# Four layers over 32 sequences: how the output of the state-space scan is multiplied by C and summed

## The chip, the cores and the metric

The kernel runs on one core of a Trainium2 chip. Its time is the device time of one execution in microseconds (us). A core has five engines that run side by side, each with its own queue that it works off in order: TensorE (PE; its weight loads are listed as PEld), VectorE (DVE), ScalarE (ACT), GpSimd (POOL) and SyncE (SP, which here only issues transfers). They wait for each other through semaphores. TensorE writes its products to PSUM, which this kernel deals out in eight banks of 512 float32 on each of 128 partitions; the other working memory is SBUF. The profile lists the clock that TensorE was granted as a share of full speed.

## The reference, cut to what matters

32 sequences (B) of 256 tokens (S) with 256 channels (D) go through four layers: a linear attention, an ordinary attention with 16 heads, a state-space layer run over time in both directions, and another linear attention. All is float32. The change is in the third layer, whose core is this:

```python
def _ssm(u, Wdbc, Wdt, bdt, Alog, Dp):           # u: 256 steps, E = 512 channels
    dlt, Bm, Cm = jnp.split(einsum(u, Wdbc), [R, R + N], axis=-1)   # R = 64, N = 16
    delta = softplus(einsum(dlt, Wdt) + bdt)
    dA  = exp(delta[..., None] * -exp(Alog))                        # N states a channel
    dBu = delta[..., None] * Bm[:, :, None, :] * u[..., None]
    h_t = dA_t * h_{t-1} + dBu_t                                    # scan over the 256 steps
    y_t = sum over n of h_t[:, n] * C_t[n]
    return y + u * Dp
...
out = (silu(mx) * (z1 + z2)) @ Wf.T + bf + skip      # z1 forward, z2 backward in time
return x + gate[:, None, :] * out
```

## The kernel before, in words

**Tiling.** Channels lie on partitions in the scans: 512 channels are 4 chunks of 128, and a tile [128, 4, 256] holds (channel, chunk, time), 1024 elements a partition. For each sequence b and direction d, `project(b, d)` makes `u`, `dbc` (64 rows for delta, then 16 rows of B and 16 of C), `dl` (delta) and `du` (delta times u). Then `scan(b, d)` takes N = 16 steps, one for each state n. So there are 32 x 2 x 16 = 1024 steps.

**One step.** TensorE copies row n of B and row n of C to all partitions (L574: two float32 matmuls with a selecting 32-row matrix, into one PSUM bank `bc`; there are two such banks). ScalarE computes `dA` with four exponentials (L580). VectorE then does three operations on 1024 elements: `du` times B (L585), the scan, a recurrence along the free dimension (L586), and the product with C in place (L587). In every odd step VectorE also adds the even step's `h` (L592), and TensorE adds the pair's sum into PSUM with an identity matrix (L594, two float32 matmuls of 512 columns, tile `ys`). After 16 steps VectorE reads the sum (L601). Each of the two `h` tiles has one buffer, so the next `h` of the same parity waits for the add and the matmul.

**What runs beside.** Two chains of other work are interleaved with the steps, by Python generators: one unit of `back(b - 1)` (the end of the state-space layer and the last layer, for the sequence before) and two of `ahead(b)` (`project(b, 1)` and then `front(b + 1)`, the first two layers and the start of the third for the next sequence). A scheduler of the framework then places the instructions in each engine's queue by its own estimate of times, so the order in a queue is not exactly that of the source. The scan of a sequence's first direction can't begin before `front` of that sequence has ended. The chains share three PSUM banks, `psG` (`bank()`); the sums of the second layer's heads, `yv` (L454), have a bank of their own, `psV`. Both chains use GpSimd for the reciprocal root in each layer norm (`stats`, L220 and L221), and for little else.

**Names that the text uses.** `ys` L594: identity matmuls that sum h; `bc` L574: broadcast of B and C; `yv` L454 and the logits L415 and L445: the second layer's heads, with 17 columns or 18 rows a matmul; `rs` L220: the norms' roots on GpSimd; L638 to L640: in `back`, the skip `xs` is added, the gate multiplied, `x` added.

Of the kernel before, what the change touches and what calls it, by code (L numbers as in the profile page):

```python
# [30 lines left out]
# Vectors that lie along the free dimension, three on each of four partitions.  # L31
# [4 lines left out]
def cond_seq_kernel(ctx: ExitStack, tc: tile.TileContext, a: dict, out: bass.AP):  # L36
    nc = tc.nc
    PSUM = bass.MemoryType.PSUM

    const = ctx.enter_context(tc.tile_pool(name="const", bufs=1))  # L40
    xin = ctx.enter_context(tc.tile_pool(name="xin", bufs=2))
    small = ctx.enter_context(tc.tile_pool(name="small", bufs=4))
# [46 lines left out]
    with tc.tile_pool(name="pre", bufs=1) as pre:  # L89
# [34 lines left out]
        # silu(cond), and its transpose  # L124
# [5 lines left out]
        ps = bank()  # L130
# [5 lines left out]
        # Half of each FiLM's scale and shift, with its norm's own folded in.  # L136
# [21 lines left out]
        # shift, scale and gate of the state space layer, a batch element a partition  # L158
# [7 lines left out]
        mod = const.tile([B, 3, D], F32, name="mod")  # L166
# [6 lines left out]
        # What the masks add to keys, and what they multiply values by.  # L173
        mb = const.tile([B, 3, S], F32, name="mb")
# [10 lines left out]
        ps = bank()  # L185
# [9 lines left out]
    # Tiles of which a part is set once and for all.  # L195
# [110 lines left out]
        # Where every key is masked, exp gives zeros and their sum's inverse no number.  # L306
# [17 lines left out]
        # queries: softmax over a head's channels, its division left to the end  # L324
# [50 lines left out]
    def attention(ch, x, b, dst):  # L375
        xT = yield from norm_T(ch, x, "ng1", "nb1")
        # A head's 16 channels of 32 partitions; row 16 pairs 1 (q) with the mask's term (k),
        # row 17 the negated maximum (q, later) with 1 (k).
        kpat = small.tile([B, P], F32, tag="kpat", name="kpat", bufs=2)
# [59 lines left out]
        for h in range(16):  # L439
            g, j = divmod(h, 4)  # L440
            hh, h8 = divmod(h, 8)
            r = slice(32 * j, 32 * j + 18)
            ps = bank()
            for m in range(2):
                nc.tensor.matmul(  # L445
                    ps[:, m * 256 : (m + 1) * 256], ka[r, g, m * P : (m + 1) * P], qa[r, g, :], start=True, stop=True
                )
            ex = wk.tile([P, 2, S], F32, tag="ex", name="ex", bufs=3)
            nc.scalar.activation(ex.rearrange("p m s -> p (m s)"), ps, AF.Exp)  # L449
            if h8 == 0:  # L450
# [13 lines left out]
            yield  # L464
# [4 lines left out]
    def front(b):  # L469
        """Layers 0 and 1, and layer 2 up to the first direction's scan."""  # L470
# [7 lines left out]
        # layer 2: norm, scale and shift, norm  # L478
        sel = ident[0:B, b : b + 1].to_broadcast([B, P])
# [3 lines left out]
        xs = wk.tile([P, 2, D], F32, tag="xs", name="xs")  # L483
# [7 lines left out]
        xn = stats("f", xs)  # L491
        yield
# [21 lines left out]
        state[b] = {"x": x2, "xs": xs, "gate": gate, "xT": xT, "mz": mz}  # L514
        yield from project(b, 0)

    def project(b, d):
        """What the scan of a direction reads; the second direction's time runs backwards."""
# [22 lines left out]
        nc.scalar.copy(dbc, ps[:96, :256])  # L541
        yield
        # softplus(z) = max(z, 0) + ln(1 + exp(-|z|))
# [20 lines left out]
        state[b][d] = (u, dbc, dl, du)  # L564
        yield

    def scan(b, d):
        u, dbc, dl, du = state[b].pop(d)
        yp = psY.tile([P, 2, 512], F32, tag="y", name="ys")
        for n in range(N):  # L570
            bc = psB.tile([P, 2, S], F32, tag="bc", name="bc")
            for i in range(2):
                o = R + i * N + n
                nc.tensor.matmul(  # L574
                    bc[:, i, :], ident[R:96, o : o + 1].to_broadcast([32, P]), dbc[R:96, :], start=True, stop=True
                )
# [8 lines left out]
            nc.vector.tensor_tensor(h, du, bc[:, 0:1, :].to_broadcast([P, 4, S]), ALU.mult)  # L585
            nc.vector.tensor_tensor_scan(hf, dA.rearrange("p c s -> p (c s)"), hf, 0.0, ALU.mult, ALU.add)  # L586
            nc.vector.tensor_tensor(h, h, bc[:, 1:2, :].to_broadcast([P, 4, S]), ALU.mult)  # L587
            # y sums over n: pairs here, the pairs in PSUM.
            if n % 2 == 0:
                even = h  # L590
            else:
                nc.vector.tensor_tensor(h, h, even, ALU.add)  # L592
                for i in range(2):
                    nc.tensor.matmul(  # L594
                        yp[:, i, :], ident, hf[:, i * 512 : (i + 1) * 512], start=n == 1, stop=n == N - 1
                    )
            yield
# [12 lines left out]
    def back(b):  # L610
        """Layer 2 from the scans on, and layer 3."""
# [30 lines left out]
        xo = wk.tile([P, 2, D], F32, tag="xo", name="xo")  # L642
# [12 lines left out]
    for b in range(B):  # L655
        # Two chains beside the scans: what remains of the last element, and the next one's start.
# [18 lines left out]
def _arrays(i):  # L675
    """The inputs as the program reads them: the same values, laid out anew."""
# [74 lines left out]
```

## Time and profile before

| | |
|---|---|
| time before, median of 3 runs | 9736.15 us (9734.44 to 9742.32) |
| the profiled execution, first to last instruction | 9737.5 us |
| PE matmul busy | 8259.0 us (85%), 27390 instructions |
| VectorE busy | 6998.2 us (72%) |
| ScalarE busy | 3321.2 us (34%) |
| GpSimd busy | 407.5 us (4%) |
| granted TensorE clock, mean | 0.693 |

One sequence takes 300 us, and the work repeats: the stretch from 4000 to 4100 us and that from 4300 to 4400 us have nearly the same busy times. In the lists of groups each row gives the line, the engine, the operation, what it writes and reads, how often, then the busy time in us, the mean of one in ns, and the idle time of the engine just before, with what ended most of it. PE busy is a modelled figure: matmuls overlap, so the spacing of their starts is the better measure of what one costs.

### The profile page before, as it was taken

The numbers are of one execution on the slowest core, as the hardware profiler recorded it, in microseconds if no ns is written. First come the engines' busy times: TensorE is split into PE (matmuls) and PEld (weight loads), VectorE is DVE, ScalarE is ACT, GpSimd is POOL, SyncE is SP. The second block draws the span as 40 slices with busy tenths as digits, with TensorE's granted clock in tenths as the row PEclk, the third lists the DMA queues.
The fourth block names the chain that finished last, engine by engine and source line by source line (L and its number), as shares of the span: only waits on it lengthen the run. The fifth ranks groups of instructions, "written<-read, shape, count | busy, mean of one in ns | idle before, by whom it ended". The sixth has DMA issues, their size and how long they took to land.

```text
span 9737.5 us, 73176 instructions
## 1 busy us (share of the span) xinstructions
PE 8259.0 (85%) x27390; PEld 5211.9 (54%) x27390; DVE 6998.2 (72%) x7756; ACT 3321.2 (34%) x7236; POOL 407.5 (4%) x557
## 2 busy tenths in 40 slices
PE   6888888888888888888888888888888888888886
PEld 4555555555555555555555555555555555555553
DVE  1777777777777777777777777777777777777776
ACT  1333332333333333323333333333233333333332
POOL 0000000000000000000000000000000000000000
PEclk6677676776666776767766667767677766677675
DMA  1000000000000000000000000000000000000000
GB/s 58 2 3 2 2 3 3 3 2 3 2 3 3 3 2 2 3 3 3 2 3 2 3 3 3 2 2 3 3 3 3 2 2 3 3 3 0 2 2 2
DMA packets 28172, 34.67 MB, mean 4 GB/s; under 512 B 3781, under 2 KB 23557, under 8 KB 27818
## 3 DMA queue, kind: packets, MB, share of 16 engines
q1 hardware_dynamic: 23024, 24.51, 0.8%
q10 hardware_dynamic: 4794, 5.49, 0.2%
q8 instruction: 217, 3.56, 0.2%
q14 instruction: 137, 1.12, 0.0%
HBM read 21.60 MB, written 8.39 MB: 3 GB/s over the span
## 4 chain that ended last, share of the span: by engine, by line
PE 66%; DVE 26%; ACT 3%; issue 2%; POOL 2%; DMA 0%; DVEq 0%; ACTq 0%; SPq 0%; POOLq 0%
PE ys L594 14%; DVE h L586 9%; PE yv L454 8%; PE g L256 7%; PE bc L574 7%; PE g L445 6%; DVE h L585 5%; PE g L257 4%; DVE h L587 4%; PE g L415 3%; PE g L390 3%; PE g L526 2%; PE g L235 2%; PE g L299 1%; PE g L550 1%
## 5 line engine op out<-in xcount | busy, mean ns | idle before, releaser
L580 ACT ACTIVATE dA<-dl,alog 128x255 f32<-128x255 f32 x4096 | 1768.0, 497 | 2320.3 <-DVE h L586 2319.8
L586 DVE TENSOR_TENSOR_SCAN h<-dA,h 128x1024 f32<-128x1024 f32 x1024 | 2337.9, 2283 | 25.4 <-ACT dA L580 1.4
L574 PE MATMUL bc<-dbc,ident 32*128 32x256 f32 x4096 | 1715.9, 553 | 682.4 <-DVE h L587 625.5
L585 DVE TENSOR_TENSOR h<-du,bc 128x1024 f32<-128x1024 f32 x1024 | 1241.6, 1212 | 1071.8 <-PE ys L594 595.5
L594 PE MATMUL ys<-h,ident 128*128 128x512 f32 x2048 | 1665.1, 957 | 301.8 <-DVE h L592 301.8
L574 PEld LDWEIGHTS bc<-dbc,ident 32*128 32x128 f32 x4096 | 967.5, 260 | 1101.1 <-issue 592.2
L587 DVE TENSOR_TENSOR h<-h,bc 128x1024 f32<-128x1024 f32 x1024 | 1240.4, 1211 | 5.8
L594 PEld LDWEIGHTS ys<-h,ident 128*128 128x128 f32 x2048 | 545.1, 296 | 1017.7 <-issue 534.6
L454 PEld LDWEIGHTS yv<-va,ex 128*128 128x128 f32 x4096 | 777.1, 283 | 348.2 <-ACT ex L449 173.3
L454 PE MATMUL yv<-va,ex 128*128 128x17 f32 x4096 | 791.7, 335 | 82.9 <-ACT ex L449 82.8
L449 ACT ACTIVATE ex<-g 128x512 f32<-128x512 f32 x512 | 294.6, 595 | 1188.0 <-PE g L445 1119.8
L415 PE MATMUL g<-ka,qa 18*128 18x256 f32 x2048 | 592.4, 569 | 78.3 <-DVE b L350 55.4
L592 DVE TENSOR_TENSOR h<-h 128x1024 f32<-128x1024 f32 x512 | 619.3, 1210 | 5.7
L445 PE MATMUL g<-qa,ka 18*128 18x256 f32 x2048 | 620.7, 557 | 0.0
L220 POOL TENSOR_SCALAR rs<-mv 128x2 f32<-128x2 f32 x256 | 204.2, 798 | 8791.9 <-DVE mv L219 8791.9
L257 PE MATMUL g<-rows,ones 1*128 1x256 f32 x1152 | 538.2, 556 | 0.0
L415 PEld LDWEIGHTS g<-ka,qa 18*128 18x128 f32 x2048 | 369.5, 269 | 235.3 <-DVE b L350 67.4
L526 PE MATMUL g<-mz,w_wc 128*128 128x256 f32 x2048 | 454.0, 380 | 0.0
L557 DVE TENSOR_SCALAR dl<-g,cols 128x256 f32<-128x256 f32 x256 | 119.9, 479 | 424.6 <-ACT ab L556 420.2
L526 PEld LDWEIGHTS g<-mz,w_wc 128*128 128x128 f32 x2048 | 390.1, 191 | 53.8 <-issue 0.6
L235 PE MATMUL g<-ident,f 128*128 128x128 f32 x896 | 216.3, 369 | 214.9 <-DVE f L224 116.3
L257 PEld LDWEIGHTS g<-rows,ones 1*128 1x128 f32 x1152 | 223.0, 240 | 266.1 <-issue 265.9
(180 smaller groups left out, 8501.5 us busy)
## 6 DMA issues: line engine op xcount, KB each, us to landing
x<-in_x_dram SPq DMA_DIRECT2D x32, 256.0 KB, 2.7
out_dram<-xo SPq DMA_DIRECT2D x32, 256.0 KB, 2.1
fw<-in_film_dram SPq DMA_DIRECT2D x3, 1024.0 KB, 10.0
wada<-in_wada_dram ACTq DMA_DIRECT2D x1, 1536.0 KB
w_wc<-in_wc_dram ACTq DMA_DIRECT2D x1, 1024.0 KB, 11.9
w_wc<-in_wc_dram SPq DMA_DIRECT2D x1, 1024.0 KB, 14.3
w_wv<-in_wv_dram ACTq DMA_DIRECT2D x2, 256.0 KB, 7.5
w_wo<-in_wo_dram ACTq DMA_DIRECT2D x2, 256.0 KB, 10.1
```

The costliest lines, as they stand in the source:

```text
L256: nc.tensor.matmul(o, xT[:, k, t * P : (t + 1) * P], w[:, k, :], start=k == 0, stop=False)
L257: nc.tensor.matmul(o, brow[1][:, :P], brow[0], start=False, stop=True)
L415: nc.tensor.matmul(ps[:, t * 256 : (t + 1) * 256], qa[r, g, t * P : (t + 1) * P], ka[r, g, :], start=True, stop=True)
L445: nc.tensor.matmul(ps[:, m * 256 : (m + 1) * 256], ka[r, g, m * P : (m + 1) * P], qa[r, g, :], start=True, stop=True)
L454: nc.tensor.matmul(yp[:, t, h8, :], ex[:, m, t * P : (t + 1) * P], va[:, m, h, :], start=m == 0, stop=m == 1)
L526: nc.tensor.matmul(ps[:, j * 256 : (j + 1) * 256], wc[d][:, k, e * P : (e + 1) * P], mz[:, k, :], start=k == 0, stop=k == 3,)
L574: nc.tensor.matmul(bc[:, i, :], ident[R:96, o : o + 1].to_broadcast([32, P]), dbc[R:96, :], start=True, stop=True)
L580: nc.scalar.activation(dA[:, c, 1:S], dl[:, c, 1:S], AF.Exp, bias=0.0, scale=aneg[d][:, c, n : n + 1])
L585: nc.vector.tensor_tensor(h, du, bc[:, 0:1, :].to_broadcast([P, 4, S]), ALU.mult)
L586: nc.vector.tensor_tensor_scan(hf, dA.rearrange("p c s -> p (c s)"), hf, 0.0, ALU.mult, ALU.add)
L587: nc.vector.tensor_tensor(h, h, bc[:, 1:2, :].to_broadcast([P, 4, S]), ALU.mult)
L594: nc.tensor.matmul(yp[:, i, :], ident, hf[:, i * 512 : (i + 1) * 512], start=n == 1, stop=n == N - 1)
```

## The change

C no longer goes through TensorE. `project` writes the 16 rows of C to a scratch in DRAM (`cd`), and `scan` reads two rows at a time back, repeated on all partitions, into an SBUF tile `cc` with three buffers. The product with C moves to GpSimd. `bc` now holds the two B rows of two steps, so there is one pair of broadcast matmuls for two steps, in a single bank. VectorE's product of `du` and B goes to a PSUM tile of two banks (`dbu`), and the scan reads it there. VectorE's add of pairs is gone: TensorE sums all 16 steps. `h` has three buffers in rotation. PSUM is dealt anew: `psB` has one bank instead of two, `psV` is gone and `yv` takes one of the three shared banks.

Smaller edits: `mod` and `mb` share one tile, on partitions 32 to 63 and 0 to 31; the buffers of `xs`, `xo`, `kpat` and of the small statistics are cut by one; and `front` now adds gate times `xs` to `x2` on GpSimd, so that `back` has two VectorE operations where it had three.

```diff
-    psB = ctx.enter_context(tc.tile_pool(name="psB", bufs=2, space=PSUM))
-    psV = ctx.enter_context(tc.tile_pool(name="psV", bufs=1, space=PSUM))
+    psB = ctx.enter_context(tc.tile_pool(name="psB", bufs=1, space=PSUM))
+    psU = ctx.enter_context(tc.tile_pool(name="psU", bufs=1, space=PSUM))
+    dram = ctx.enter_context(tc.tile_pool(name="dram", bufs=2, space=bass.MemoryType.DRAM))
...
-                yp = psV.tile([P, 2, 8, 17], F32, tag="v", name="yv")
+                yp = bank()[:, : 2 * 8 * 17].rearrange("p (t h d) -> p t h d", t=2, h=8)
...
         xn = stats("f", xs)
+        nc.gpsimd.tensor_tensor(xs, xs, gate.unsqueeze(1).to_broadcast([P, 2, D]), ALU.mult)
+        nc.gpsimd.tensor_tensor(x2, x2, xs, ALU.add)
...
+        cd = dram.tile([N, S], F32, tag="cd", name="cd")
+        nc.sync.dma_start(out=cd, in_=dbc[R + N : R + 2 * N, :])
...
         for n in range(N):
-            bc = psB.tile([P, 2, S], F32, tag="bc", name="bc")
-            for i in range(2):
-                o = R + i * N + n
-                nc.tensor.matmul(
-                    bc[:, i, :], ident[R:96, o : o + 1].to_broadcast([32, P]), dbc[R:96, :], start=True, stop=True
-                )
+            if n % 2 == 0:
+                cc = big.tile([P, 2, S], F32, tag="cc", name="cc", bufs=3)
+                nc.sync.dma_start(out=cc, in_=cd[n : n + 2, :].partition_broadcast(P))
+                bc = psB.tile([P, 2, S], F32, tag="bc", name="bc")
+                for i in range(2):
+                    o = R + n + i
+                    nc.tensor.matmul(
+                        bc[:, i, :], ident[R:96, o : o + 1].to_broadcast([32, P]), dbc[R:96, :], start=True, stop=True
+                    )
...
-            h = big.tile([P, 4, S], F32, tag=f"h{n % 2}", name="h", bufs=1)
+            h = big.tile([P, 4, S], F32, tag="h", name="h", bufs=3)
             hf = h.rearrange("p c s -> p (c s)")
-            nc.vector.tensor_tensor(h, du, bc[:, 0:1, :].to_broadcast([P, 4, S]), ALU.mult)
-            nc.vector.tensor_tensor_scan(hf, dA.rearrange("p c s -> p (c s)"), hf, 0.0, ALU.mult, ALU.add)
-            nc.vector.tensor_tensor(h, h, bc[:, 1:2, :].to_broadcast([P, 4, S]), ALU.mult)
-            if n % 2 == 0:
-                even = h
-            else:
-                nc.vector.tensor_tensor(h, h, even, ALU.add)
-                for i in range(2):
-                    nc.tensor.matmul(
-                        yp[:, i, :], ident, hf[:, i * 512 : (i + 1) * 512], start=n == 1, stop=n == N - 1
-                    )
+            dbu = psU.tile([P, 4, S], F32, tag="dbu", name="dbu")
+            j = n % 2
+            nc.vector.tensor_tensor(dbu, du, bc[:, j : j + 1, :].to_broadcast([P, 4, S]), ALU.mult)
+            nc.vector.tensor_tensor_scan(
+                hf, dA.rearrange("p c s -> p (c s)"), dbu.rearrange("p c s -> p (c s)"), 0.0, ALU.mult, ALU.add
+            )
+            nc.gpsimd.tensor_tensor(h, h, cc[:, j : j + 1, :].to_broadcast([P, 4, S]), ALU.mult)
+            for i in range(2):
+                nc.tensor.matmul(
+                    yp[:, i, :], ident, hf[:, i * 512 : (i + 1) * 512], start=n == 0, stop=n == N - 1
+                )
...
-        nc.vector.tensor_tensor(x3, ps.rearrange("p (c d) -> p c d", c=2), s["xs"], ALU.add)
-        nc.vector.tensor_tensor(x3, x3, s["gate"].unsqueeze(1).to_broadcast([P, 2, D]), ALU.mult)
+        nc.vector.tensor_tensor(
+            x3, ps.rearrange("p (c d) -> p c d", c=2), s["gate"].unsqueeze(1).to_broadcast([P, 2, D]), ALU.mult
+        )
         nc.vector.tensor_tensor(x3, x3, s["x"], ALU.add)
```

More of the change, by code (lines that the diff above doesn't have):

```diff
@@ L41, in cond_seq_kernel @@
     xin = ctx.enter_context(tc.tile_pool(name="xin", bufs=2))
-    small = ctx.enter_context(tc.tile_pool(name="small", bufs=4))
+    small = ctx.enter_context(tc.tile_pool(name="small", bufs=3))
     psY = ctx.enter_context(tc.tile_pool(name="psY", bufs=1, space=PSUM))
-    psB = ctx.enter_context(tc.tile_pool(name="psB", bufs=2, space=PSUM))
-    psV = ctx.enter_context(tc.tile_pool(name="psV", bufs=1, space=PSUM))
+    psB = ctx.enter_context(tc.tile_pool(name="psB", bufs=1, space=PSUM))
+    psU = ctx.enter_context(tc.tile_pool(name="psU", bufs=1, space=PSUM))
+    dram = ctx.enter_context(tc.tile_pool(name="dram", bufs=2, space=bass.MemoryType.DRAM))
     psG = ctx.enter_context(tc.tile_pool(name="psG", bufs=3, space=PSUM))
@@ L165, in cond_seq_kernel @@
             nc.vector.tensor_copy(ada[:, lo : lo + n], ps[:B, :n])
-        mod = const.tile([B, 3, D], F32, name="mod")
+        mm = const.tile([2 * B, 3, D], F32, name="mm")
+        mod, mb = mm[B : 2 * B], mm[0:B]
         nc.vector.tensor_scalar(ada[:, 256:512], ada[:, 256:512], 1.0, None, ALU.add)
@@ L171, in cond_seq_kernel @@
         nc.vector.tensor_copy(mod[:, 2, :], ada[:, 512:768])
-        mb = const.tile([B, 3, S], F32, name="mb")
         mv_ = pre.tile([B, 3, S], F32, name="mvalid")
@@ L376, in attention @@
         xT = yield from norm_T(ch, x, "ng1", "nb1")
-        kpat = small.tile([B, P], F32, tag="kpat", name="kpat", bufs=2)
+        kpat = small.tile([B, P], F32, tag="kpat", name="kpat", bufs=1)
         nc.gpsimd.tensor_scalar(kpat, pat, ident[0:B, b : b + 1], None, ALU.mult)
@@ L477, in front @@
         yield from attention("f", x1, b, x2)
-        sel = ident[0:B, b : b + 1].to_broadcast([B, P])
+        sel = ident[B : 2 * B, B + b : B + b + 1].to_broadcast([B, P])
         xh = stats("f", x2)
@@ L482, in front @@
         nc.tensor.matmul(gh, sel, mod[:, 0:2, :].rearrange("b i d -> b (i d)"), start=True, stop=True)
-        xs = wk.tile([P, 2, D], F32, tag="xs", name="xs")
+        xs = wk.tile([P, 2, D], F32, tag="xs", name="xs", bufs=1)
         nc.vector.tensor_tensor(xs, xh, gh[:, 0:256].unsqueeze(1).to_broadcast([P, 2, D]), ALU.mult)
@@ L513, in front @@
             yield
-        state[b] = {"x": x2, "xs": xs, "gate": gate, "xT": xT, "mz": mz}
+        state[b] = {"x": x2, "gate": gate, "xT": xT, "mz": mz}
         yield from project(b, 0)
@@ L563, in project @@
         nc.vector.tensor_tensor(du, dl, u, ALU.mult)
-        state[b][d] = (u, dbc, dl, du)
+        state[b][d] = (u, dbc, cd, dl, du)
         yield
     def scan(b, d):
-        u, dbc, dl, du = state[b].pop(d)
+        u, dbc, cd, dl, du = state[b].pop(d)
         yp = psY.tile([P, 2, 512], F32, tag="y", name="ys")
         for n in range(N):
-            bc = psB.tile([P, 2, S], F32, tag="bc", name="bc")
-            for i in range(2):
-                o = R + i * N + n
-                nc.tensor.matmul(
-                    bc[:, i, :], ident[R:96, o : o + 1].to_broadcast([32, P]), dbc[R:96, :], start=True, stop=True
-                )
+            if n % 2 == 0:
[7 more added lines that the diff above has]
+                    )
             dA = dA_tiles[n % 2]
@@ L637, in back @@
         x3 = wk.tile([P, 2, D], F32, tag="x3", name="x3", bufs=1)
-        nc.vector.tensor_tensor(x3, ps.rearrange("p (c d) -> p c d", c=2), s["xs"], ALU.add)
-        nc.vector.tensor_tensor(x3, x3, s["gate"].unsqueeze(1).to_broadcast([P, 2, D]), ALU.mult)
+        nc.vector.tensor_tensor(
+            x3, ps.rearrange("p (c d) -> p c d", c=2), s["gate"].unsqueeze(1).to_broadcast([P, 2, D]), ALU.mult
+        )
         nc.vector.tensor_tensor(x3, x3, s["x"], ALU.add)
         yield
-        xo = wk.tile([P, 2, D], F32, tag="xo", name="xo")
+        xo = wk.tile([P, 2, D], F32, tag="xo", name="xo", bufs=1)
         yield from linear_attention("b", x3, 3, 2, b, w3, 8, 1, xo, True)
```

## The prediction

> **What bounds the kernel now.** I read the page's first table, then the chain of work that ended last, then the groups of instructions, then the busy times in stretches of one sequence.
>
> ```profile
> PE 8259.0 (85%) x27390; PEld 5211.9 (54%) x27390; DVE 6998.2 (72%) x7756; ACT 3321.2 (34%) x7236; POOL 407.5 (4%) x557
> ...
> PE 66%; DVE 26%; ACT 3%; issue 2%; POOL 2%; DMA 0%; DVEq 0%; ACTq 0%; SPq 0%; POOLq 0%
> ...
> L574 PE MATMUL bc<-dbc,ident 32*128 32x256 f32 x4096 | 1715.9, 553 | 682.4 <-DVE h L587 625.5
> L585 DVE TENSOR_TENSOR h<-du,bc 128x1024 f32<-128x1024 f32 x1024 | 1241.6, 1212 | 1071.8 <-PE ys L594 595.5
> L594 PE MATMUL ys<-h,ident 128*128 128x512 f32 x2048 | 1665.1, 957 | 301.8 <-DVE h L592 301.8
> L587 DVE TENSOR_TENSOR h<-h,bc 128x1024 f32<-128x1024 f32 x1024 | 1240.4, 1211 | 5.8
> L592 DVE TENSOR_TENSOR h<-h 128x1024 f32<-128x1024 f32 x512 | 619.3, 1210 | 5.7
> ```
>
> No engine is full. The chain is on PE for 66% of the span and on DVE for 26%, and the two wait for each other: PE's broadcast for the C product (L574 on L587), DVE's next product for the sum (L585 on L594). To see which side ends last where, I took stretches of 20 us. Columns: length, then busy us and instructions of PE, PEld, DVE, ACT, POOL, then the granted clock.
>
> ```profile
> 4300.00:4320.00 20.00, 19.28 (x89) 14.91 (x90) 15.57 (x13) 7.04 (x15) 0.00 (x0) 0.59 0.00 1
> 4342.00:4362.00 20.00, 15.93 (x34) 7.85 (x33) 16.10 (x17) 6.53 (x15) 1.80 (x2) 0.59 0.01 1
> 4362.00:4382.00 20.00, 10.55 (x20) 4.45 (x20) 16.28 (x28) 1.39 (x3) 2.77 (x6) 0.51 0.00 0
> ```
>
> The first lies in the heads of layer two: PE is full. The last two lie in the norms behind it: PE has holes, DVE sets the pace. In all three the clock is near half. What that does shows where an instruction group of `ys` ran alone:
>
> ```profile
> 4006.80:4010.20 3.40, 3.40 (x8) 1.61 (x8) 3.11 (x4) 1.45 (x3) 0.00 (x0) 0.60 0.00 0
> 4010.20:4013.60 3.40, 2.68 (x27) 2.24 (x26) 3.40 (x3) 2.04 (x6) 0.00 (x0) 0.90 0.00 0
> 4026.80:4030.20 3.40, 3.40 (x6) 1.47 (x6) 0.00 (x0) 2.18 (x5) 0.00 (x0) 0.53 0.00 0
> 4030.20:4033.60 3.40, 2.65 (x19) 2.16 (x17) 3.25 (x3) 0.60 (x1) 0.00 (x0) 0.97 0.00 0
> ```
>
> The four instructions of one `ys` group fill 3.4 us at half clock, and the 3.4 us after them run at 0.90 and 0.97. I went through such groups from 4000 to 4300 us: of 12 that began cold, 9 were followed by a fast stretch.
>
> Last, a pair of steps with no other work beside it, near the end of the run (timeline of DVE: start, us, instruction):
>
> ```profile
> 9641.21 1.22 DVE L585 TENSOR_TENSOR h<-du,bc 128x1024 f32<-128x1024 f32 x1
> 9642.53 2.29 DVE L586 TENSOR_TENSOR_SCAN h<-dA,h 128x1024 f32<-128x1024 f32 x1
> 9645.44 1.22 DVE L585 TENSOR_TENSOR h<-du,bc 128x1024 f32<-128x1024 f32 x1 [0.61 <-PE ys L594]
> 9646.58 1.21 DVE L587 TENSOR_TENSOR h<-h,bc 128x1024 f32<-128x1024 f32 x1
> 9647.71 2.28 DVE L586 TENSOR_TENSOR_SCAN h<-dA,h 128x1024 f32<-128x1024 f32 x1
> 9650.03 1.22 DVE L587 TENSOR_TENSOR h<-h,bc 128x1024 f32<-128x1024 f32 x1
> 9651.28 1.22 DVE L592 TENSOR_TENSOR h<-h 128x1024 f32<-128x1024 f32 x1
> 9652.61 1.22 DVE L585 TENSOR_TENSOR h<-du,bc 128x1024 f32<-128x1024 f32 x1
> ```
>
> 11.4 us a pair, nearly all of it DVE work in a row.
>
> [...]
>
> **PE, part by part.** In the `ys` groups at half clock weight loads start 0.85 us apart (4007.65, 4008.51, 4009.36), so 512 columns cost 0.853 us cold and half that, 0.427, warm; 256 columns 0.213 warm (L526 on the chain: 32 in 6.91 us, 0.216 each); short ones, `yv` among them, 0.107 (16 in 1.85 us in a warm stretch). The groups list holds 18368 of 256 columns, 2112 of 512 and 6784 short ones, which makes 3918 + 901 + 724 = 5543 us at full clock. At clock 0.693 that is 7999 us, so PE is in use for 82% of the span and idle for 1739 us. The change takes away 2048 broadcast instructions (-437) and adds 2048 `ys` instructions (+874): 5980 us. Clock times use must be above 5980/9737.5 = 0.614 for a gain; it is 0.569 now. At clock and use unchanged the time would be 10,505 us.
>
> **DVE.** 1024 x 1.211 (L587) and 512 x 1.210 (L592) go, with one operation of 0.69 us in `back` for each sequence: -1882 us, from 6998 to 5116. L585 and L586 stay in number. Writing to and reading from PSUM instead of SBUF isn't shown by the trace; L585 already reads PSUM at the 1212 ns of an SBUF-only product (L592 1210). I [...]take 0.
>
> **POOL.** [...] Its queue is in order, so each of the 256 norm roots (now 0.8 + 0.7 us) can sit behind a product that waits for its scan: [...]1.5 taken, and half of it shows: 8 x 1.5/2 = 6 us a sequence at most, 4 taken, since PE often has other work.
>
> **DMA.** For each scan a 16 KB write, and 8 reads of 256 KB. Loads of that size land in 2.7 us (`x`), stores in 2.1 us. Between the copy of `dbc` and the first product lie PE, ACT and DVE work of more than 8 us (chain at 4097.26 to 4107), and three buffers give two pairs of lead, over 14 us. In SP's queue the reads stand with the loads of `x` and stores of `out`, two a sequence. I take 0; if the cover were gone, 5 us for each of 64 scans, 320 us.
>
> **By stage, a sequence of 300 us.** I counted matmuls by shape in fifteen stretches of 20 us. In six of them (from 4122, 4142, 4182, 4322, 4342, 4362) PE use (that work over length times clock) is 52 to 73%; they have 42 of the 53 us of PE idle, 15 scans, 106 us of DVE and 48.1 us of PE at full clock. After the change: DVE 106 - 15 x 1.82 = 79; PE 57.5, at these stretches' own clocks 93 us. So PE becomes the bound there; with 13 us left idle for the latency of norms 106 us, which saves 14. In the other nine PE is used for 82 to 100%; they gain about 5 us of PE work, at 0.72 clock +7. Then the clock: 16 more `ys` groups a sequence, each with 9/12 chance to bring a fast 3.4 us if it begins cold (0.61 of the time): 16 x 0.45 x 3.4 = 24 us, of which I take three quarters, as DVE limits the rest: -18. GpSimd's delay +4. Sum: -14 + 7 - 18 + 4 = -21 us a sequence, -672 in all: 9737.5 - 672 = 9065. Execution and median agree within 2 us, so I say 9060: clock times use 0.660, say 0.73 and 0.90.
>
> Costed at nothing: the single `bc` bank (free after the second product, needed after a scan of 2.3 us; without PE time in that gap up to 2 us for 512 pairs, 1000 us, but then PE is late, not idle), the lost bank in the heads (PE full there, two banks suffice for a 0.6 us exponential), smaller pools. The 595.5 us in which L585 waited for `ys` become a wait of the scan for the third-last `h`.
>
> **Rivals.**
> 1. Slower: `ys` holds up PE. It now stands in PE's queue for every step, behind scan and GpSimd, and all chain matmuls stand behind it. For it: 130 waits of PE and its weight loads on L592 now (list of waits). Against it: PE is behind elsewhere. My forecast leaves 9060 - 5980/0.73 = 870 us idle; 0.66 us more for each of 1024 steps eats the gain. At 1 us: 10,080; range 9760 to 10,500. Chance 0.22.
> 2. Faster than forecast: with PE always fed, `ys` runs keep the clock up also between heads. Clock 0.80 at use 0.90: 5980/0.72 = 8306. For it: stretches with dense products run at 0.91 to 1.00 (4082 to 4122). Against it: `yv` and logits stay cold even at full PE. Chance 0.20.
> 3. GpSimd is the bound: that needs 8.8 us a product[...]. 0.02, near 10,500.
> 4. The gains cancel: 9740. 0.03.
>
> **Numbers.** Forecast 8700 to 9700, chance 0.53. Faster 0.74, within 0.2% (about what this measurement can tell from no change) 0.03, slower 0.23. The range goes from 8400, which cuts off half of rival 2, to 9850, which takes in the start of rival 1.
>
> **What would show it.** Mean clock 0.71 to 0.76; PE on more than 75% of the chain; DVE near 5100 us; [...]few waits of POOL on `cc`. Wrong if the clock stays at 0.69, or if PE's idle time before L604 (`ys`) grows past 700 us.

## The result, and the profile after

The changed kernel takes 9609.75 us (median of 4 runs, 9604.46 to 9614.48) against 9738.27 us for the kernel before beside it: a ratio of 0.9869, 95% interval 0.9855 to 0.9883. It is faster by 1.3%, where 9060 us, 6.9% less, was forecast. The direction held and the time lies in the range that was given, but four fifths of the expected gain are missing.

The page of the changed kernel, its first table and the groups that answer to those shown of before. Columns of a group: busy us and mean ns of one, then idle time before it and what ended most of it.

```profile
PE 8215.6 (86%) x27390; PEld 4901.7 (51%) x27390; DVE 5590.8 (58%) x6188; ACT 3315.1 (35%) x7236; POOL 2825.2 (29%) x1645
...
L602 POOL TENSOR_TENSOR h<-h,cc 128x1024 f32<-128x1024 f32 x1024 | 2461.9, 2404 | 5720.2 <-DVE h L599 2264.9
L604 PE MATMUL ys<-h,ident 128*128 128x512 f32 x4096 | 2800.2, 821 | 747.7 <-POOL h L602 747.6
...
L599 DVE TENSOR_TENSOR_SCAN h<-dA,dbu 128x1024 f32<-128x1024 f32 x1024 | 2336.5, 2282 | 78.3 <-ACT dA L591 18.4
L598 DVE TENSOR_TENSOR dbu<-du,bc 128x1024 f32<-128x1024 f32 x1024 | 1254.6, 1225 | 1808.0 <-PE bc L585 1793.3
...
L237 PE MATMUL g<-ident,f 128*128 128x128 f32 x896 | 184.4, 308 | 249.4 <-DVE f L226 237.2
```

VectorE lost a fifth of its work and GpSimd took the product at 2.40 us each. PE waits 747.7 us in front of the sum (L604), 301.8 before, and VectorE 1793.3 us for the broadcast of B (L598). The mean granted clock went from 0.693 to 0.805. The chain of waits of this profile breaks off after 1% of the span, so nothing is read from it.

The prediction split a time into PE's work at full clock, divided by the mean clock, and the rest, PE's idle time. The table below makes the same split of profiled executions (work counted as there). It is rough: the clock is a mean over the whole span, and "idle" is all that the split leaves. The page, which counts each matmul to its modelled end, has PE without work for only 1389 us after, 1478 before and 1014 in e4. With each matmul weighed at the clock of its own start, an estimate from the traces, idle time is 1942, 1537 and 1431 us. So only differences of some hundred us between kernels that do the same work are read from it.

| kernel | work, us | clock | work / clock | idle | span |
|---|---|---|---|---|---|
| before | 5543 | 0.693 | 7999 | 1739 | 9737.5 |
| forecast | 5980 | 0.73 | 8192 | 870 | 9060 |
| after | 5980 | 0.805 | 7429 | 2176 | 9604.9 |
| e4 (C on VectorE) | 5980 | 0.803 | 7447 | 1650 | 9096.6 |

Against the forecast the clock gives 763 us more and the idle time takes 1306 us more. So the question is why so much more is left idle than was forecast.

The timeline of after, where steps run with nothing beside them, near the end of the run (start, us, engine and instruction; in brackets the idle time before and its cause):

```profile
9509.64 1.12 PE L585 MATMUL bc<-dbc,ident 32*128 32x256 f32 x4
...
9510.80 1.23 DVE L598 TENSOR_TENSOR dbu<-du,bc 128x1024 f32<-128x1024 f32 x1 [3.59 <-PE bc L585]
...
9512.16 2.29 DVE L599 TENSOR_TENSOR_SCAN h<-dA,dbu 128x1024 f32<-128x1024 f32 x1
...
9514.58 2.35 POOL L602 TENSOR_TENSOR h<-h,cc 128x1024 f32<-128x1024 f32 x1 [4.88 <-issue]
9515.84 2.29 DVE L599 TENSOR_TENSOR_SCAN h<-dA,dbu 128x1024 f32<-128x1024 f32 x1
...
9516.99 3.78 PE L604 MATMUL ys<-h,ident 128*128 128x512 f32 x4 [4.31 <-POOL h L602]
...
9520.70 2.07 PE L585 MATMUL bc<-dbc,ident 32*128 32x256 f32 x4
...
9522.80 1.23 DVE L598 TENSOR_TENSOR dbu<-du,bc 128x1024 f32<-128x1024 f32 x1 [4.67 <-PE bc L585]
```

The shown pair of before took 11.4 us, nearly all of it VectorE's work. This one takes 12.0 us (9510.80 to 9522.80), although VectorE works for only 7.0 of them (two of 1.23 and two of 2.29). The even scan ends at 9514.5, GpSimd's product at 9516.9, the sum takes PE until 9520.8 at half clock (0.50 granted from 9516.99 to 9520.77), the next broadcast of B stands behind it in PE's queue, and VectorE waits 4.67 us for that. GpSimd's product has become a link of a chain that runs through PE's queue. This pair is the slowest of the four in a row that run alone here: the three before it, from 9479.70, take 9.3, 10.9 and 10.9 us, at a clock of 0.82 to 0.84 where this one has 0.73. So the chain's length hangs on the clock as well, and a pair on its own is not slower than before on the whole; what is missing is most of what VectorE's shorter work could have brought.

GpSimd also slows VectorE. Timeline again, a norm beside a product, and the same operation alone 19 us later:

```profile
4003.48 2.75 DVE L226 TENSOR_SCALAR f<-f,mv,rs 128x256 f32<-128x256 f32 x2
4003.70 2.37 POOL L602 TENSOR_TENSOR h<-h,cc 128x1024 f32<-128x1024 f32 x1 [1.37 <-PE ys L604]
...
4006.28 0.55 PE L237 MATMUL g<-ident,f 128*128 128x128 f32 x3 [1.96 <-DVE f L226]
...
4022.39 0.73 DVE L226 TENSOR_SCALAR f<-x,mv,rs 128x256 f32<-128x256 f32 x2 [2.63 <-POOL rs L223]
```

Two norm operations take 0.73 us alone and 2.75 us here: the second ends only with GpSimd's product (4006.23 and 4006.07), and PE waits 1.96 us for it. By tile, four kinds of VectorE operation are longer than before (number times mean): `f<-f,mv,rs` 52.4 to 175.0 us in all (128 of 0.41 us, then of 1.37), `b<-b,b` 43.7 to 108.0, `du` 77.6 to 109.9, `x<-x,x` 21.9 to 47.4; 245 us together. L598 and L599 are not: 1225 and 2282 ns, where before had 1212 and 2283. Each of these two takes one of its inputs from PSUM; e2 below gives the scan both from SBUF. How a product on GpSimd lengthens an operation of VectorE these runs don't show.

### The profile page after: what moved, and what is told of

The parts are those of the page before. It is cut to its first block, busy times and chain, and to the rows that moved or that the text cites. A ratio compares the mean times of both kernels' runs of the same rounds, so it can differ in the third digit from the quotient of the medians.

```text
span 9604.9 us, 74808 instructions
## 1 busy us (share of the span) xinstructions
PE 8215.6 (86%) x27390; PEld 4901.7 (51%) x27390; DVE 5590.8 (58%) x6188; ACT 3315.1 (35%) x7236; POOL 2825.2 (29%) x1645
## 5 line engine op out<-in xcount | busy, mean ns | idle before, releaser
L602 POOL TENSOR_TENSOR h<-h,cc 128x1024 f32<-128x1024 f32 x1024 | 2461.9, 2404 | 5720.2 <-DVE h L599 2264.9
L604 PE MATMUL ys<-h,ident 128*128 128x512 f32 x4096 | 2800.2, 821 | 747.7 <-POOL h L602 747.6
L599 DVE TENSOR_TENSOR_SCAN h<-dA,dbu 128x1024 f32<-128x1024 f32 x1024 | 2336.5, 2282 | 78.3 <-ACT dA L591 18.4
L598 DVE TENSOR_TENSOR dbu<-du,bc 128x1024 f32<-128x1024 f32 x1024 | 1254.6, 1225 | 1808.0 <-PE bc L585 1793.3
L604 PEld LDWEIGHTS ys<-h,ident 128*128 128x128 f32 x4096 | 905.3, 244 | 1868.7 <-POOL h L602 972.4
L456 PEld LDWEIGHTS g<-va,ex 128*128 128x128 f32 x4096 | 773.4, 276 | 411.1 <-issue 213.7
L456 PE MATMUL g<-va,ex 128*128 128x17 f32 x4096 | 749.9, 324 | 86.4 <-ACT ex L451 86.4
L585 PE MATMUL bc<-dbc,ident 32*128 32x256 f32 x2048 | 691.3, 455 | 0.0
L417 PE MATMUL g<-ka,qa 18*128 18x256 f32 x2048 | 452.4, 451 | 180.3 <-DVE mneg L420 122.9
L585 PEld LDWEIGHTS bc<-dbc,ident 32*128 32x128 f32 x2048 | 388.9, 212 | 286.8 <-issue 247.0
L447 PEld LDWEIGHTS g<-qa,ka 18*128 18x128 f32 x2048 | 415.7, 266 | 70.2 <-DVE qa L434 1.9
L237 PE MATMUL g<-ident,f 128*128 128x128 f32 x896 | 184.4, 308 | 249.4 <-DVE f L226 237.2
L237 PEld LDWEIGHTS g<-ident,f 128*128 128x128 f32 x896 | 114.7, 151 | 396.1 <-issue 276.6
```

Of the source, the lines that this page charges most:

```text
L417: nc.tensor.matmul(ps[:, t * 256 : (t + 1) * 256], qa[r, g, t * P : (t + 1) * P], ka[r, g, :], start=True, stop=True)
L447: nc.tensor.matmul(ps[:, m * 256 : (m + 1) * 256], ka[r, g, m * P : (m + 1) * P], qa[r, g, :], start=True, stop=True)
L456: nc.tensor.matmul(yp[:, t, h8, :], ex[:, m, t * P : (t + 1) * P], va[:, m, h, :], start=m == 0, stop=m == 1)
L585: nc.tensor.matmul(bc[:, i, :], ident[R:96, o : o + 1].to_broadcast([32, P]), dbc[R:96, :], start=True, stop=True)
L598: nc.vector.tensor_tensor(dbu, du, bc[:, j : j + 1, :].to_broadcast([P, 4, S]), ALU.mult)
L602: nc.gpsimd.tensor_tensor(h, h, cc[:, j : j + 1, :].to_broadcast([P, 4, S]), ALU.mult)
```

## The experiments

All ratios are to the kernel before, run on the same chip. A kernel without a diff of its own is the changed kernel with the edit named.

### Which part took the gain: C's product

**e4, C on VectorE.**

```diff
-            nc.gpsimd.tensor_tensor(h, h, cc[:, j : j + 1, :].to_broadcast([P, 4, S]), ALU.mult)
+            nc.vector.tensor_tensor(h, h, cc[:, j : j + 1, :].to_broadcast([P, 4, S]), ALU.mult)
```

> The product with C goes back to VectorE, reading cc from SBUF; GpSimd has only the norms' roots. Theory Q: one link less between scan and sum, but 1240 us more DVE work; PE's idle before ys goes down to 300 us or less, time 9500 to 9800. Theory that GpSimd's share of the gain is what there is (DVE's load decides): 9900 to 10300.

Measured 9092.11 us (9077.83 to 9098.43), ratio 0.9334 [0.932, 0.9348]: 518 us under the changed kernel, although VectorE has 1,024 operations more, and below what either theory expected. The page:

```profile
PE 8082.2 (89%) x27390; PEld 4774.3 (52%) x27390; DVE 6435.9 (71%) x7212; ACT 3313.6 (36%) x7236; POOL 367.3 (4%) x621
...
L604 PE MATMUL ys<-h,ident 128*128 128x512 f32 x4096 | 2852.9, 836 | 502.6 <-DVE h L602 500.1
```

PE waits 245 us less for the sum, at the same clock (0.803). All of the gain is in the idle time (table above).

**e9, no product with C at all** (L602 and the load of `cc` are gone, so C is missing from the output).

> No product with C at all, on any engine, and no load of cc: C is left out of the output, the sum takes h from the scan. Theory: the full GpSimd product costs in two ways, about 350 us by its place between scan and sum (9610 to 9263 when only that was taken away) and about 400 us by its load on queue[...]. Then this run, with neither, lies at 8750 to 8950, by the run with the short product. If it stays above 9100, the load costs little and the short run gained by something else, such as another order of the queues.

Measured 9008.24 us, 0.9246 [0.923, 0.9261], between the two expectations. So on VectorE C's product costs 84 us, on GpSimd 602. From its page:

```profile
PE 8150.0 (90%) x27390; PEld 4896.2 (54%) x27390; DVE 5344.7 (59%) x6188; ACT 3307.7 (37%) x7236; POOL 365.5 (4%) x621
...
L596 DVE TENSOR_TENSOR dbu<-du,bc 128x1024 f32<-128x1024 f32 x1024 | 1254.7, 1225 | 1662.5 <-PE bc L583 1642.4
```

VectorE has the same 6,188 operations as in the changed kernel and is busy for 246 us less, which confirms the 245 us above. It still waits 1642 us for the broadcast, so most of that long wait doesn't come from GpSimd's product.

**e8, the product on 16 of 256 columns (first diff); e7, the full product into a tile that nobody reads, in bfloat16 and with one buffer of `cc` less so that it fits (second).** Both leave most or all of C out of the output.

```diff
-            nc.gpsimd.tensor_tensor(h, h, cc[:, j : j + 1, :].to_broadcast([P, 4, S]), ALU.mult)
+            nc.gpsimd.tensor_tensor(
+                h[:, :, 0:16], h[:, :, 0:16], cc[:, j : j + 1, 0:16].to_broadcast([P, 4, 16]), ALU.mult
+            )
```

```diff
-                cc = big.tile([P, 2, S], F32, tag="cc", name="cc", bufs=3)
+                cc = big.tile([P, 2, S], F32, tag="cc", name="cc", bufs=2)
...
-            nc.gpsimd.tensor_tensor(h, h, cc[:, j : j + 1, :].to_broadcast([P, 4, S]), ALU.mult)
+            hc = big.tile([P, 4, S], mybir.dt.bfloat16, tag="hc", name="hc", bufs=1)
+            nc.gpsimd.tensor_tensor(hc, h, cc[:, j : j + 1, :].to_broadcast([P, 4, S]), ALU.mult)
```

> GpSimd multiplies only the first 16 of each 256 columns, so that most of the product with C is left out of the output; the chain through GpSimd stays, but is 2 us shorter a step[...]. If the length of the product in the chain[...] is the cost: 9000 to 9200. If it is the extra handover between engines as such: 9400 to 9600.

> GpSimd makes the same product each step, but into a tile that nobody reads (bfloat16, to fit; cc has two buffers instead of three), and the sum takes h straight from the scan: C is left out of the output. GpSimd is as busy as before[...] but the chain from scan to sum no longer goes through it. If GpSimd's place in that chain is the cost: 9000 to 9250 or less. If [...]the norms' roots queued behind products are the cost: 9450 to 9650.

e8: 8848.17 us, 0.9105 [0.9071, 0.9139], faster than either theory expected; the product now takes 373 ns. e7: 9262.69 us, 0.9515 [0.9499, 0.9531], just above the range of the first theory. Shortening the link gains 762 us, taking it out of the chain, with the full product left on GpSimd, gains 347. But e8 is 160 us faster than e9, which does less. By the split above most of that is the clock: 5980 us of work take 7328 us at e8's 0.816 and 7466 at e9's 0.801. Something else than the work moves by such amounts. A candidate is the framework's scheduler, which places every instruction anew for each kernel; the last group of runs holds the order.

**e10, even steps on GpSimd, odd steps on VectorE.**

> The C product of odd steps on VectorE, of even steps on GpSimd. If the cost grows with each GpSimd product: half way between 9610 and 9092, 9300 to 9400. If VectorE's free time makes a mixture best: 9050 or less. If any GpSimd product spoils the pair: 9500 or more.

Measured 9517.15 us, 0.9772 [0.9757, 0.9786]: half of the products back on VectorE bring 93 of the 518 us, not half (the third expectation).

### The other parts

**e11, the sums alone**: the kernel before, without the add of pairs and with TensorE summing every step.

```diff
-            if n % 2 == 0:
-                even = h
-            else:
-                nc.vector.tensor_tensor(h, h, even, ALU.add)
-                for i in range(2):
...
+            for i in range(2):
+                nc.tensor.matmul(
+                    yp[:, i, :], ident, hf[:, i * 512 : (i + 1) * 512], start=n == 0, stop=n == N - 1
+                )
```

> The kernel before with one part of the change alone: VectorE's add of pairs is gone and TensorE sums every step (874 us more PE work at full clock, 619 us less DVE). If the sums raise the clock as in the changed kernel: clock 0.75 or more, time 9300 to 9700. If the clock's rise came from the other parts: clock about 0.70 and 10200 us or more.

Measured 9956.65 us, 1.0222 [1.0207, 1.0238], slower. The clock is 0.777 in place of 0.693, as the first theory had it, but the time isn't. Its work is 5543 + 874 = 6417 us, or 8259 at that clock. The 874 us would be 1261 at the clock of before; PE's work grew by 260 (7999 to 8259). So by this count the sums pay for most of themselves through the clock, and not for all. The drop of PE's work to 7429 us in the changed kernel then goes with the broadcasts that are gone and a clock that is higher still; no run takes the broadcasts away alone. VectorE's wait for the broadcast rises from 464.8 us to 1553.2 here, so it comes with the sums and needs no product on GpSimd.

**e2, the product with B in SBUF again** (written to `h`, scanned in place; the two banks stay unused), **and e3, the same with `psB` at two banks.**

```diff
-            nc.vector.tensor_tensor(dbu, du, bc[:, j : j + 1, :].to_broadcast([P, 4, S]), ALU.mult)
+            nc.vector.tensor_tensor(h, du, bc[:, j : j + 1, :].to_broadcast([P, 4, S]), ALU.mult)
...
-                hf, dA.rearrange("p c s -> p (c s)"), dbu.rearrange("p c s -> p (c s)"), 0.0, ALU.mult, ALU.add
+                hf, dA.rearrange("p c s -> p (c s)"), hf, 0.0, ALU.mult, ALU.add
```

> The product with B is written to h in SBUF and scanned in place; the two PSUM banks of dbu are left unused. DVE's scan then has two SBUF inputs while GpSimd multiplies. If the place in PSUM keeps the two engines apart, scan and GpSimd product stretch (2.28 and 2.40 us now) by 1 to 2 us and the time goes to 9800 to 10300; if the place means nothing, both stay and so does 9610 within 50 us.

> As the run with the product in SBUF, with a second bank for bc. Theory B (the single bc bank is what DVE waits for: 1793 us): 300 us or more below the run with one bank, with DVE's waits for bc under 700 us. Theory Q or L: within 100 us of it, because the broadcast comes late in PE's queue and not for want of a bank.

e2: 9955.88 us, 1.0219 [1.0202, 1.0236], in the range expected if PSUM matters, though with less stretch than the 1 to 2 us thought of. The groups of its page:

```profile
L600 POOL TENSOR_TENSOR h<-h,cc 128x1024 f32<-128x1024 f32 x1024 | 2769.6, 2711 | 5714.1 <-DVE h L597 3822.0
L602 PE MATMUL ys<-h,ident 128*128 128x512 f32 x4096 | 2980.2, 870 | 985.1 <-POOL h L600 980.5
L597 DVE TENSOR_TENSOR_SCAN h<-dA,h 128x1024 f32<-128x1024 f32 x1024 | 2478.8, 2434 | 17.7 <-ACT dA L590 1.6
```

With both scan inputs in SBUF, scan and product lengthen each other: 2434 ns for 2282 and 2711 for 2404. The PSUM tile is worth 346 us in a kernel that has GpSimd at work (the order that changes with it included). e3: 9805.08 us, 1.0068 [1.0053, 1.0083]: with a second `bc` bank the kernel is 151 us faster there, between the two expectations (new order included; the clock is 0.791 for 0.782).

### Where the sum and the broadcast stand in the queue

**e1, each sum emitted a step later; e12, that with C on VectorE.** `add` holds the two matmuls that the diff takes away.

```diff
-            for i in range(2):
-                nc.tensor.matmul(
-                    yp[:, i, :], ident, hf[:, i * 512 : (i + 1) * 512], start=n == 0, stop=n == N - 1
-                )
+            if late is not None:
+                add(*late)
+            late = (n, hf)
```

> The sum of a step (ys) is emitted one step later than in the changed kernel; all else is as there. Theory Q (PE's queue holds the sum in front of other work while GpSimd still multiplies, and the next broadcast of B stands behind it): PE's 748 us before ys and most of the 1793 us of DVE's waits for bc go, the time falls to 8700 to 9200 us. Theory L (with PE now at 0.8 of its clock, the chains' own latency, norm, transpose, projection one after another, sets the pace): less than 100 us of gain, 9500 to 9650, and the idle time moves to other matmuls.

> C product on VectorE and the sum emitted one step later. PE waits 500 us in front of ys in the run with C on VectorE. If that is worth something: 8800 to 9000, the best with a full output. If, as with GpSimd, idle time only moves to the chains: 9050 to 9150.

e1: 9576.42 us (9535 to 9649), 0.9841 [0.9792, 0.989]; the range takes in that of the changed kernel, so no gain is shown. PE's idle time before the sum falls by 288 us to 460. Part of it moved: the waits of L237 for VectorE rise by 160 us (for the norm L226 from 237.2 to 324.5, for L319 from 8.6 to 81.6). And the clock falls to 0.757. By the split, idle time falls by 428 us in the profiled execution and work over clock rises by 471. e12: 9346.24 us, 0.9601 [0.9587, 0.9615], 254 us slower than e4, which neither expectation had: the clock is 0.760, work over clock rises by 421 us and idle time falls by 148.

**e5, the next pair's broadcast emitted right behind the odd product with B; e6, that with C on VectorE.** `spread` holds the two matmuls of L585.

```diff
+            if j == 1 and n < N - 1:
+                bc = spread(n + 1)
```

> The changed kernel with the next pair's broadcast of B emitted right behind the odd step's product with B, ahead of that step's GpSimd product and sum. In the changed kernel that broadcast starts 9.95 us (mean) after it could, and DVE waits 1793 us for it. Theory B-late (the broadcast's place in PE's queue is what costs the gain): wait under 900 us, time 9000 to 9250, near the run with the C product on VectorE (9092). Theory G (GpSimd's own length in the chain, its queue[...] is the cost): under 100 us of gain, 9500 to 9620.

> The C product on VectorE and the early broadcast together. Theory B-late: the wait of VectorE's product for bc (897 us in the run with C on VectorE alone) halves, 8800 to 9000. Theory G: nothing more to gain from the broadcast, 9050 to 9150.

e5: 9791.72 us, 1.0056 [1.0041, 1.0071]: 182 us slower than the changed kernel, which neither theory had. VectorE's wait for `bc` hardly fell:

```profile
DVE dbu L604 <- PE bc L583: 1598.1, 200, 15.2
```

So e5 doesn't say what that wait of 1793 us costs; e9, which keeps 1642 us of it in a kernel 602 us faster, shows that it isn't where GpSimd's cost lies. Here too the clock falls (0.766): work over clock rises by 378 us, idle time falls by 193. e6: 9053.25 us (9043.66 to 9080.69), 0.9303 [0.9286, 0.9319], the fastest kernel here that computes the whole; its range overlaps e4's, as theory G expected.

In e1, e5 and e12 an edit that takes idle time from PE thus also lowers its clock, and the clock takes all of it and more. Why the clock falls was not tested.

### The engine or the order: queues held fixed

**m1 to m4: every engine issues in the order in which the program was written.** The changed kernel, C on VectorE as in e4, the short product as in e8, and the unread one as in e7, each with

```diff
-        cond_seq_kernel(tc, args, out)
+        with tc.manual_schedule():
+            cond_seq_kernel(tc, args, out)
```

> The changed kernel with every engine's queue in the order in which the program writes its instructions, so that the framework's scheduler chooses nothing. It is the base for the three that run beside it, and slower than the changed kernel itself in either theory: 9,900 to 11,500 us, because each product with B now stands directly behind the sum of the step before. Theory 'length' (the 2.4 us product between scan and sum[...] cost the time): PE's idle time before the sum's matmuls stays the largest wait, above 700 us. Theory 'order' (the queue that the scheduler made for this kernel was an unlucky one): nothing certain of this run alone; what counts is its distance to the next.

> The same pinned order with C's product on VectorE, so that PE's and ScalarE's queues are those of m1 to the instruction. Theory 'length': 400 to 900 us under m1, about the 518 us between the two when the scheduler ordered them, or more. Theory 'order': within 150 us of m1.

> m1 with GpSimd's product cut to 16 of 256 columns (0.37 us in place of 2.4); the rest of C's product is left out, so the output isn't the reference's. 512 products shorter by 2.0 us is 1,040 us if each stands in the chain. Theory 'length': 700 to 1,300 us under m1, and under m2 by 200 us or more. Theory 'order': 0 to 300 us under m1.

> m1 with GpSimd's product at its full length but written to a tile that nobody reads, while the sum takes the scan's state: C is left out of the output. [...] Theory 'length' with the chain as the larger part: 500 to 1,100 us under m1 and within 350 us above m3.[...] Theory 'order': within 300 us of m1 and of m3.

m1 took 18032.8 us, m2 16733.07, m3 16053.63, m4 15434.0 (ratios 1.8515, 1.7181, 1.6484, 1.5847, each within 0.003). The level was badly misjudged: in written order each step waits for the one before through PE's queue (1,017 waits before the sum). (The 512 products in m3's text are a slip; there are 1,024.) The differences are clean:

| from m1 | link shorter by | times 1,024 | measured |
|---|---|---|---|
| to m2, C on VectorE | 2.38 + 0.14 - 1.22 - 0.03 = 1.27 us | 1300 us | 1300 us |
| to m3, short | 2.38 - 0.36 = 2.02 us | 2068 us | 1979 us |
| to m4, out of the chain | 2.38 + 0.14 = 2.52 us | 2580 us | 2599 us |

(0.14 us is the gap from scan to product on GpSimd, 0.03 on VectorE.) The groups of m1 and then of m4:

```profile
L604 PE MATMUL ys<-h,ident 128*128 128x512 f32 x4096 | 3821.9, 1088 | 7640.6 <-POOL h L602 7640.6
```

```profile
L605 PE MATMUL ys<-h,ident 128*128 128x512 f32 x4096 | 3805.9, 1084 | 5081.8 <-DVE h L599 5081.8
```

The difference of the two waits, 2559 us, is nearly the whole gain of 2599. The three gains lie above the ranges expected; theory 'length' holds in this order: a product in front of a sum that PE waits for costs its full length and its hand-over, and one that stands beside the chain costs nothing that shows here. What the product does to VectorE's own operations m1 and m4 don't tell apart: VectorE is busy for 5602.1 us in m1 and 5605.9 in m4 with the same 6,188 operations, and for 5426.9 in m3, with the short product.

**p1 and p2: the scheduler's own orders, exchanged.** Order-only edges along TensorE's, ScalarE's and VectorE's queues hold the changed kernel to the order made for e4 (p1), and e4 to the order made for the changed kernel (p2); the 1,024 products and the queues of GpSimd and SyncE are left to the scheduler. In the traces, ScalarE and VectorE (its products aside) run in exactly the order of the model, TensorE but for 12 (p1) and 84 (p2) of 27,390 places.

```diff
+    traced = {i.name: i for i in nc.cur_bb.bb.instructions}
...
+                tc.add_manual_dep(
+                    ins, prev.name,
+                    mybir.DependencyInfo(mybir.DependencyClass.NoSync, mybir.DependencyReason.DATA),
+                    reason="pinned order",
+                )
```

> The changed kernel, with C's product on GpSimd, whose TensorE, ScalarE and VectorE queues are held by order-only edges to the very order that the framework's scheduler chose for e4 (C on VectorE); the 1,024 products are the only instructions on another engine. Changed kernel: 9,610 us, e4: 9,092. Theory 'engine' (what GpSimd's product adds to the chain and takes from VectorE costs the 518 us, whatever the order): 9,500 to 9,800 us, and PE's idle time before the sum stays above 650 us. Theory 'order' (the scheduler, given the slower product, chose a worse order): 9,050 to 9,250 us, PE's idle time before the sum near e4's 500 us. Halfway, 9,250 to 9,500, means that both share it in that measure.

> e4 (C's product on VectorE) with its TensorE, ScalarE and VectorE queues held to the order that the scheduler chose for the changed kernel; only the place of the 1,024 products in VectorE's queue is left to the scheduler. Theory 'engine': 9,000 to 9,250 us. Theory 'order': 9,450 to 9,650 us. With the run beside it this makes a table of two engines by two orders: the difference along each side is what that side costs.

| | order made for GpSimd's product | order made for VectorE's product |
|---|---|---|
| C on GpSimd | 9609.75 (after) | 9583.5 (p1), 0.984 [0.9828, 0.9853] |
| C on VectorE | 9643.09 (p2), 0.9899 [0.9871, 0.9927] | 9092.11 (e4) |

Neither theory holds alone: p1 came out as "engine" expected, p2 as "order" did. In e4's order GpSimd's product costs 491 us; in the other, taking it off GpSimd gains nothing. What PE and VectorE waited for most, first in p1, then in p2 (us, times, longest):

```profile
PE ys L607 <- POOL h L605: 712.7, 388, 5.1
...
DVE dbu L601 <- PE bc L588: 1318.6, 291, 17.6
```

```profile
PE ys L607 <- DVE h L605: 601.7, 436, 4.0
...
DVE dbu L601 <- PE bc L588: 1213.7, 251, 12.5
```

In e4 these are 500.1 and 896.8 us, in the changed kernel 747.6 and 1793.3. Part of both losses is the clock, 0.777 in p1 and 0.782 in p2 against e4's 0.803: by the split 249 of p1's 482 us over e4, 200 of p2's 541 (profiled executions). A queue that was laid out for one length of the product does worse with the other. Both halves, the short link and the order planned for it, are needed for the 518 us. It isn't the products' own place that p2 pays for: they start 0.31 us after their scans, in e4 0.48 (means). How the wait of p2 comes about, step by step, was not traced.

## Why the prediction was right in sign and wrong in size

**The step that failed** is the cost of GpSimd's product in the stage sum ("GpSimd's delay +4" us a sequence, 128 us in all), and with it the use of 0.90 that left 870 us idle. It priced GpSimd by the roots in its own queue alone, at 1.5 us each, a figure that the author assumed. The product's place in front of each sum was left to rival 1. In the runs C's product on GpSimd costs 602 us over none (e9) and 518 over VectorE (e4), order and clock included; PE's idle time is 2176 us. The time stayed in the range by luck: a clock better than forecast made up for 763 of the 1306 us.

**Rival 1** ("`ys` holds up PE") described this, with its point of decision: 0.66 us more for each of 1024 steps eats the gain. PE's idle time is 1306 us above the forecast's, 1.28 us a step, and its idle time before L604 passed the 700 us that the prediction named as its refutation. It still didn't make the kernel slower, as its price assumed the clock of the forecast.

**The clock** came out at 0.805, not 0.73: right in direction (more `ys` groups, more warm time), too small by 0.075, worth 763 us. e11 shows that the sums raise it without the rest (0.777). Two stretches of after, with the columns of those shown of before, the second in the heads of layer two:

```profile
4142.00:4162.00 20.00, 17.92 (x67) 10.91 (x67) 11.35 (x15) 7.73 (x18) 5.63 (x4) 1.00 0.10 27
...
4242.00:4262.00 20.00, 19.75 (x52) 13.54 (x53) 3.42 (x5) 5.16 (x12) 4.22 (x2) 0.50 0.04 14
```

These are the ends of a row of eight stretches from 4122 us. In the first, beside scans, the clock is full (1.00), while VectorE, busy for 11.35 of 20 us, no longer sets the pace, as the stage sum said. In the second, in the heads, the clock is half (0.50) although PE is busy for 19.75 of 20 us. So being busy isn't enough for the full clock in the heads; what would be enough there these stretches don't show. Rival 2 had this clock, with a use that the product didn't allow: 0.623/0.805 = 0.77 in place of 0.90 (0.623 is 5980/9604.9). That e4 lands within 0.4% of 9060 us is thus no proof of the sum: there too the clock is higher than forecast and the idle time 780 us more.

**VectorE** was to fall to 5116 us and fell to 5590.8. The durations of all its operations, added up singly, are 7476 us before and 5873 after. That they fall by 1603 and not by 1882 is due to longer operations, 279 us, 245 of them in the four kinds that meet GpSimd's product. The other 196 us are overlaps of neighbours: the page counts such time once, and the forecast subtracted it in full. The forecast left out what GpSimd's product does to the norms on VectorE.

**Right:** PSUM for the product with B at no cost on VectorE (+13 ns), with the scan at 2282 ns for 2283, where e2 with SBUF has 2434; transfers hidden (`cc` lands in 3.3 us, and the trace names no wait of GpSimd for it); GpSimd not the bound (2.40 us a product, 29% busy). The norms' roots start 0.39 us (mean) after their input in place of 0.09, 77 us over 256 roots: less than the 1.5 us each that the sum took, so it was not the roots that GpSimd's product held up most.

**Costed at nothing, and not shown to be free:** the single bank of `bc`. In e3 the second bank goes with 151 us, new order included, in a kernel where the product with B is in SBUF; for the changed kernel itself there is no bank left, so its price there stays open. The bank that the heads lost is open too: PE's wait for `mneg` before the logits rose from 22.2 us to 122.9, but is 28.5 in e4, which has no more banks.

**Stays open:** what the longer operations of VectorE cost alone, and what sets the mean clock. e7, with the full product on GpSimd, and e8, with one of 373 ns, differ by 414 us, but also in their order and clock.

## What to carry to other kernels

An engine that is far from full can still be the wrong place for an operation: if PE's in-order queue has an instruction that waits for it, its length can count in every step, as in m1 (2.02 us less a step, in m3, gave 1979 us over 1,024 steps), and everything queued behind waits too, so price the link first and the engine's load second. Before moving work from VectorE to GpSimd, list which operations of VectorE will run beside it, and which engine waits for those. Here `f<-f,mv,rs` went from 0.41 to 1.37 us, and in e2 the scan with both inputs in SBUF from 2282 to 2434 ns; with one input in PSUM, product and scan stayed within 13 ns of before. Where a scheduler lays out the queues, a small edit's time includes a new order: hold the order and exchange it before believing a difference of a few per cent, and read the clock beside each idle time, as the one can take back what the other gains (in e1 428 us less idle, 471 more for the work).

## What was not expected of the hardware

TensorE's mean clock rose from 0.693 to 0.805 with 8% more work, and stood at 0.757 to 0.816 in e1 to e12, whose queues the scheduler laid out; it was 0.64 to 0.68 in m1 to m4, where PE waited in nearly every step. Two norm operations of VectorE stretched from 0.73 to 2.75 us beside one product of GpSimd. And the order of the same instructions alone moved e4 by 551 us (p2).
